# A two-layer network with causal attention on one core: the short score packs of two sequences in column tiles in one PSUM bank, and the sending of probabilities placed between the two halves of the query move

## The chip, the core and the metric

The kernel runs on one core of a Trainium2 chip. The metric is device time in microseconds (us), one launch, float32 throughout. An execution has five engines that each work through their own queue in order: TensorE (PE in the profile; PEld is its weight load), VectorE (DVE), ScalarE (ACT), GpSimd (POOL), and SyncE (SP), which here only issues transfers. Data lies in SBUF (128 partitions); matmuls write PSUM, eight banks of 128 x 512 float32.

## The reference, cut to what matters

Two layers act on 16 sequences of 256 tokens with 256 features. The first (a linear recurrence gated by an MLP) is not touched by the change. The second multiplies an attention output by a gate and adds it to x:

```python
q = (x @ Wq).reshape(B, S, 16, 192)          # 128 "nope" + 64 rotated columns per head
c_kv, k_rope = split(x @ Wkv_a, [64])        # 64 latent + 64 rotated columns, shared by all heads
k, v = expand(rmsnorm(c_kv) @ Wkv_b)         # per head
scores = einsum('bqhd,bkhd->bhqk', q, k) / sqrt(192)
scores = where(tril, scores, -max)
out = einsum('bhqk,bkhd->bqhd', softmax(scores), v) @ Wo
x = x + out * silu(base(x) + lora(x))
```

The kernel folds the expansion of the keys into the query weights, so a score is a product over 128 numbers: 64 latent and 64 rotated ones (two rotated halves of 32). All heads share the same keys of a sequence.

## The kernel before, in words

Tokens are worked in 8 chunks of 512, that is two sequences (b = 0 and 1) each. In the second layer a chunk has 16 heads in 4 groups of 4. A *unit* is one group of heads and one sequence; there are 64 units, and the main loop runs over them: step i works on unit i, sequence 0 in even steps and sequence 1 in odd ones. r is the step's place in its chunk (0 to 7). Units 2n and 2n+1 make group n.

**Scores.** The 256 queries of a sequence are cut into 8 blocks of 32. Block a of 4 heads is one matmul with 4 x 32 = 128 weight columns; because of the causal mask it meets only the first 32(a+1) keys. The 8 matmuls go in three packs, each into one PSUM bank (`PACK`): blocks 7 and 6; blocks 5, 4 and 3; blocks 2, 1 and 0, which have 96, 64 and 32 columns. The three packs of a unit are spread over its step (`score_pack`, lines 1671, 1706 and 1722), with other matmuls between them. A float32 matmul is two passes, so that pack 2 of a unit is 6 instructions at full width. From unit 6 on, the even units do pack 2 differently: each block as two matmuls with 64 weight columns, one for the lower and one for the upper half of the output partitions (`halves`), 12 instructions, marked 128\*64 in the profile. Odd units do pack 2 at full width. After the matmuls of a pack, DVE adds the mask and takes the row maxima (`nm`), ACT takes exponentials into a buffer `pr` (one for even, one for odd units) and sums the rows (`sr`); later DVE takes the reciprocals and POOL multiplies (`normalise`): packs 0 and 1 at the end of the step, pack 2 at the start of the next. The pool of score banks has 3 banks, that of all other matmul outputs 5.

**Probabilities.** The next step transposes them on DVE (`turn`, three calls; the last, `turn(w, 0)`, stands after pack 1 of the step). `send` (4 transfers) writes them to memory outside the core (`far`), and `fetch` reads them back as `pT` with the heads arranged for the product with the values: per group 4 fetches, (y, b) for key half y and sequence b. `values_of(n)` multiplies both sequences of a group at once, 32 matmuls in quarters of the array (64\*64), first with y = 0, then with y = 1. It stands in even step 2n + 4, after pack 1. So group n is sent in steps 2n+1 (sequence 0) and 2n+2 (sequence 1), fetched in steps 2n+2 and 2n+3, and used in step 2n+4.

**Queries.** Group n is projected in steps 2n-3 and 2n-2 (`query_mm`); POOL combines the rotated halves (`query_rot`, tile `qrot`), and `query_move` copies them to partitions 64 to 127 of `qg` with 8 transfers, 4 for each rotated half. This stands first in even step 2n-2, and the scores of group n begin in step 2n.

**The SP queue.** Moves, sends and fetches of the main loop are all issued by SP, in program order; each waits for what it needs before the next is issued. In an even step the order is: 8 moves, fetch (0, 0), 4 sends of the odd unit before, fetch (1, 0); in an odd step: fetches (0, 1) and (1, 1), then 4 sends of the even unit.

PE's order is the program's: a manual dependency chains each instruction to the one before it. After the last step a tail computes the last products and writes the last rows.

Of the kernel before, what the change touches and what calls it, by code (L numbers as in the profile page):

```python
# [11 lines left out]
F32 = mybir.dt.float32  # L12
# [6 lines left out]
P = 128  # L19
B, S, D = 16, 256, 256  # L20
NTOK = B * S
CH = 512
# [19 lines left out]
def tile_two_layers(ctx: ExitStack, tc: tile.TileContext, d: dict, out: bass.AP):  # L42
# [54 lines left out]
    pe = InOrder(nc.tensor)  # L97
# [132 lines left out]
    chunks = [Chunk() for _ in range(NCH)]  # L230
# [150 lines left out]
    NQ = S // 32  # L381
# [4 lines left out]
    groups = [Group() for _ in range(NCH * NG)]  # L386
# [40 lines left out]
        gp.tensor_tensor(q.rot[:, 0, :], m0[:, 0, :], m1_[:, 1, :], ALU.subtract)  # L427
        gp.tensor_tensor(q.rot[:, 1, :], m1_[:, 0, :], m0[:, 1, :], ALU.add)

    def query_move(n):  # L430
        q = groups[n]
        for r in range(2):
            for h in range(G):
                sp.dma_start(
                    q.qg[64 + 32 * r : 96 + 32 * r, :, h, :],
                    q.rot[32 * h : 32 * h + 32, r, :].rearrange("p (a q) -> p a q", q=32),
                )


    with ExitStack() as l0:  # L440
# [106 lines left out]
        def tiny(name, n=1):  # L547
            return w0.tile([P, n], F32, tag=name, name=name)
# [43 lines left out]
        u = tiny("u")  # L592
        f = tiny("f")
# [24 lines left out]
        for k in range(8):  # L618
            n = 1 << k
# [112 lines left out]
        def recur_in(ch, pb):  # L732

            v = a2.tile([P, S], F32, tag="v", name=f"v_{ch}")
            w = a2.tile([P, S], F32, tag="w", name=f"w_{ch}")
            v0.tensor_tensor(v, pb, ct, ALU.mult)
            swapped(w, pb)
            return v, w
# [8 lines left out]
        def recur_out(ch, g, w, ve, ge):  # L747

            swapped(w, g)
            h = a2.tile([P, S], F32, tag="hs", name=f"hs_{ch}")  # L750
            ve.tensor_tensor(h, g, ct, ALU.mult)
            ge.tensor_tensor(h, h, w, ALU.subtract)
            return h
# [478 lines left out]
        o = out1  # L1232
        for ch in range(FIRST, NCH - 1):
            xn, xnT, norm2, o = middle(ch, xn, xnT, norm2, fill, o)
# [25 lines left out]
        v, w = recur_in(ch, recur_mm(ch, xnT, ps_mm))  # L1260
# [7 lines left out]
        h = recur_out(ch, g, w, v0, g0)  # L1268
# [33 lines left out]
    ps_sc = ctx.enter_context(tc.tile_pool(name="ps_sc", bufs=3, space=PSUM))  # L1302
# [37 lines left out]
    PACK = (((7, 0), (6, 256)), ((5, 0), (4, 192), (3, 384)), ((2, 0), (1, 96), (0, 192)))  # L1340
# [12 lines left out]
    for t in prs:  # L1353
        for a in range(NQ):
            w = 32 * (a + 1)
# [3 lines left out]
    class Unit:  # L1359


        def __init__(self, i):
            self.i = i
            self.ch, r = divmod(i, 2 * NG)
            self.g, self.b = divmod(r, 2)
            self.n = f"{self.ch}_{self.g}_{self.b}"
            self.pr = prs[i % NPR]

    def score_pack(u, pi):
        k, b, pack = chunks[u.ch], u.b, PACK[pi]  # L1370
        if pi == 0:
            u.nm = sm1.tile([P, NQ], F32, tag="nm", name=f"nm_{u.n}", bufs=3)
            u.sr = sm1.tile([P, NQ], F32, tag="sr", name=f"sr_{u.n}", bufs=3)
        qg = groups[u.i // 2].qg
        sc = ps_sc.tile([P, CH], F32, tag="sc", name=f"sc_{u.n}_{pi}")
        halves = 2 if pi == 2 and u.b == 0 and u.i > 4 else 1
        m = P // halves
        for a, o in pack:
            w = qg[:, b * NQ + a, :, :].rearrange("p h q -> p (h q)")
            for y in range(halves):  # L1380
                pe.matmul(
                    sc[m * y : m * y + m, o : o + 32 * (a + 1)], w[:, m * y : m * y + m],
                    k.kT[:, b * S : b * S + 32 * (a + 1)], start=True, stop=True,
                )
        ends = [o + 32 * (a + 1) for a, o in pack]
        step = ends[1] - ends[0]
        n = len(pack)
        assert ends == [ends[0] + step * z for z in range(n)]
        if ends[0] - 32 + step * n <= CH:
            diag = sc[:, ends[0] - 32 : ends[0] - 32 + step * n].rearrange("p (n s) -> p n s", n=n)[:, :, 0:32]  # L1390
        else:
            diag = sc[:, ends[0] - step : ends[-1]].rearrange("p (n s) -> p n s", n=n)[:, :, step - 32 : step]
        ve.tensor_tensor(diag, diag, bc(kmask, n), ALU.add)
        for a, o in pack:
            ve.tensor_reduce(
                u.nm[:, a : a + 1], sc[:, o : o + 32 * (a + 1)], AX.X, ALU.max, negate=True
            )
        for a, o in pack:
            w = 32 * (a + 1)
            ac.activation(  # L1400
                u.pr[:, OFF[a] : OFF[a] + w], sc[:, o : o + w], AF.Exp,
                bias=u.nm[:, a : a + 1], accum_out=u.sr[:, a : a + 1],
            )

    def normalise(u, packs):
        blocks = [a for pi in packs for a, _ in PACK[pi]]
        lo, hi = min(blocks), max(blocks) + 1
        ve.reciprocal(u.sr[:, lo:hi], u.sr[:, lo:hi])
        for a in blocks:
            v = u.pr[:, OFF[a] : OFF[a] + 32 * (a + 1)]  # L1410
            gp.tensor_scalar(v, v, u.sr[:, a : a + 1], 1.0, ALU.mult, ALU.mult)
# [32 lines left out]
    def fetch(n, y, b):  # L1444

        q = groups[n]
        if y == b == 0:
            q.pT = {}
        if b == 0:
            q.pT[y] = pp.tile([P, G, 3 * P], F32, tag="pT", name=f"pT_{n}_{y}", bufs=3)  # L1450
        sp.dma_start(
            q.pT[y][64 * b : 64 * b + 64].rearrange("p h q -> p (h q)"),
            q.far[b].rearrange("(y k) s h z q -> y (k s) (h z q)", y=2)[y],
        )
# [197 lines left out]
    units = [Unit(i) for i in range(LAST)]  # L1652
    for i in range(LAST):
        ch, r = divmod(i, PER)
        odd = i % 2 == 1
        u, w = units[i], units[i - 1] if i else None
        here = w is not None and w.i >= LAST - 2
        n = (i + 3) // 2 if odd else (i + 2) // 2
        n = n if n < len(groups) else None
        more = ch + 1 < NCH  # L1660
        last = ch - 1 if ch == NCH - 1 and r in FINISH else None
        fast = ch - 1 if 0 < ch < NCH - 1 else None

        if not odd and n is not None:
            query_move(n)
        if odd and i > 2:
            fetch((i - 3) // 2, 0, 1)
            fetch((i - 3) // 2, 1, 1)
        elif i and not odd:
            fetch((i - 2) // 2, 0, 0)  # L1670
        score_pack(u, 0)
        if w:
            normalise(w, (2,))
        if fast is not None and r > 3:
            fast_begin(fast, r)
        if ch > 1 and r == 0:
            fast_begin(ch - 2, 0)
        out_weights(i)
        if r == 1:
            gate_end(ch, 0)  # L1680
        if r == 2:
            gate_end(ch, 1)
            if more and ch:
                norm_end(ch + 1)
        if r == 5 and more:
            kv_end(ch + 1)
        if i == LAST - 1:

            finish_mm(last, 3, 0, NPAIR)
            finish_out(last, 3)  # L1690
            last = None
        if w:
            for z in (1, 2):
                turn_here(w, z) if here else turn(w, z)

        if r == 0:
            mid_chunk(ch)
        if r == 7 and more:
            key_chunk(ch + 1)
        if n is not None:  # L1700
            query_mm(n, 0 if odd else 3)
            if not odd:
                query_lat(n, 3)
        if i == 5:
            values_of(0)
        score_pack(u, 1)

        if odd and n is not None:
            query_mm(n, 1)
            query_mul(n, 0)  # L1710
        if w:
            if here:
                turn_here(w, 0)
            else:
                turn(w, 0)
                send(w)
        if not odd:
            if i > 4:
                values_of((i - 4) // 2)
            if i:  # L1720
                fetch((i - 2) // 2, 1, 0)
        score_pack(u, 2)
        normalise(u, (0, 1))

        if odd and n is not None:
            query_mm(n, 2)
            query_mul(n, 1)
            query_rot(n)
            query_lat(n, 2)
        if r < 2:  # L1730
            gate_begin(ch, r)
        if r == 0 and more and ch:
            norm_begin(ch + 1)
        if r == 2 and more:
            transpose_chunk(ch + 1)
        if r == 4 and more:
            kv_begin(ch + 1)
        if r == 6 and more:
            router_chunk(ch + 1)
        if last is not None:  # L1740
            j = FINISH.index(r)
            finish_mm(last, j, 0, NPAIR)
            finish_out(last, j)
        if fast is not None and r in FINISH:
            fast_end(fast, r)
# [1 line left out]

    ch = NCH - 1
    u0, u1 = units[LAST - 2], units[LAST - 1]
    normalise(u1, (2,))  # L1750

    finish_mm(ch, 0, 0, 4)
    finish_mm(ch, 1, 0, 4)
# [86 lines left out]
```

## Time and profile before

| | us |
|---|---|
| median of 3 runs | 906.04 (905.31 to 906.72) |
| the profiled execution | 903.67 |
| its span, first to last instruction | 901.9 |
| PE busy | 889.3 (99%) |
| DVE, POOL, ACT busy | 667.4, 571.2, 476.0 |
| first score matmul | at 266.5 |
| last score matmul | at 877.2 |

The span is from the first to the last instruction that the profile records; the execution's own time is 1.8 us longer. A group's line gives operation, output and inputs, the shape, the count, then busy time, mean duration in ns and the idle time before. Matmuls overlap in a pipeline: a duration is not what a matmul adds to the queue, which is the distance from its start to the start of the next. So costs on PE are read from starts in the timeline. The mean granted clock of PE over the span is 0.994.

### The profile page before, as it was taken

To read this page: it belongs to the slowest core of one execution; us is meant where nothing else is said; L and a number is where in the kernel's file an instruction comes from. 1 tells how busy PE (TensorE), PEld (TensorE's weight loads), DVE (VectorE), ACT (ScalarE), POOL (GpSimd) and SP (SyncE) were. 2 spreads that over 40 slices of the span, in tenths; PEclk is the share of its full clock that TensorE was granted. 3 is DMA by queue.
4 is the path that set the end of the run, shared out by engine and by line. 5 is a ranking of instruction groups with operands and counts; after the bars stand their busy time and mean duration, and the time that the engine had idled before them with its cause. 6 is when DMAs were issued, how large, how long until landed. Compare 5 with 4: busy or idle time off the path is not lost.

```text
span 901.9 us, 17976 instructions
## 1 busy us (share of the span) xinstructions
PE 889.3 (99%) x5688; PEld 666.8 (74%) x5688; DVE 667.4 (74%) x2017; ACT 476.0 (53%) x1562; POOL 571.2 (63%) x885
## 2 busy tenths in 40 slices
PE   9999999999999989999999999999999999999988
PEld 8777999987757657776776777677677767766766
DVE  6886678764687869678868867886886788687642
ACT  3234665644436646655655565565556556556441
POOL 2229687787355537787586677758667775876531
PEclk9999999999999999999999999999999999999989
DMA  9730000000024888887887887788788768878880
GB/s 276 245 118 1 1 2 1 1 1 1 1 32 79 230 209 198 186 207 161 217 218 169 206 181 201 180 217 214 170 200 211 190 170 209 210 176 194 209 223 29
DMA packets 197406, 134.04 MB, mean 149 GB/s; under 512 B 143104, under 2 KB 187968, under 8 KB 197312
## 3 DMA queue, kind: packets, MB, share of 16 engines
q1 hardware_dynamic: 195184, 128.69, 58.0%
q0 software_dynamic: 1152, 3.67, 1.2%
q8 instruction: 46, 0.75, 0.4%
q10 hardware_dynamic: 976, 0.53, 0.2%
q14 instruction: 48, 0.39, 0.1%
HBM read 63.11 MB, written 52.95 MB: 129 GB/s over the span
## 4 chain that ended last, share of the span: by engine, by line
PE 93%; DVE 3%; DMA 2%; POOL 1%; ACT 1%; SPq 0%; issue 0%; ACTq 0%; POOLq 0%
PE pq L53 23%; PE sc L53 14%; PE po L53 11%; PE av L53 8%; PE f L53 7%; PE r L53 7%; PE pg L53 5%; PE ph L53 5%; PE pf L53 5%; PE pm L53 2%; PE pkv L53 2%; PE tp L53 2%; DMA far<-turned 1%; DMA pT<-far 1%; PE pb L53 1%; PE py L53 1%
## 5 line engine op out<-in xcount | busy, mean ns | idle before, releaser
L53 POOL TENSOR_SCALAR pr<-pr,sr 128x256 f32<-128x256 f32 (+7 forms) x512 | 192.5, 397 | 188.2 <-DVE sr L53 180.3
L53 ACT ACTIVATE pr<-sc,nm 128x256 f32<-128x256 f32 (+7 forms) x512 | 190.2, 382 | 217.1 <-DVE sr L53 139.6
L53 PEld LDWEIGHTS sc<-kT,qg 128*128 128x128 f32 (+1 forms) x1198 | 150.8, 176 | 54.8 <-issue 41.6
L53 PE MATMUL sc<-kT,qg 128*128 128x32 f32 (+6 forms) x1198 | 169.0, 290 | 0.0
L53 DVE TENSOR_REDUCE nm<-sc 128x1 f32<-128x256 f32 (+7 forms) x512 | 127.5, 301 | 6.6
L53 DVE STREAM_TRANSPOSE turned<-pr 128x512 f32<-128x512 f32 x186 | 123.2, 687 | 11.0 <-POOL pr L53 10.9
L53 PE MATMUL pq<-xnT,wlat 128*128 128x512 f32 x256 | 122.7, 602 | 0.0
L53 PE MATMUL pq<-xnT,wrope 128*128 128x512 f32 x256 | 120.2, 593 | 0.0
L53 ACT ACTIVATION_READ_ACCUMULATOR pr<-sc,nm 128x1 f32 x512 | 104.0, 203 | 0.0
L53 PE MATMUL av<-pT,rowv 64*64 64x512 f32 (+2 forms) x992 | 80.5, 445 | 6.0 <-DMA pT<-far 6.0
L53 POOL TENSOR_TENSOR qrot<-qmul,qmul 128x512 f32<-128x512 f32 x64 | 83.6, 1329 | 2.8 <-DVE qmul L53 2.8
L53 DVE TENSOR_TENSOR sc<-sc,kmask 128x96 f32<-128x96 f32 (+1 forms) x192 | 45.2, 236 | 53.8 <-PE sc L53 52.5
L53 DVE TENSOR_TENSOR qmul<-pq,rot_q 128x512 f32<-128x512 f32 x128 | 80.7, 672 | 0.1
L53 ACT ACTIVATE qg<-pq 64x512 f32<-64x512 f32 x128 | 75.5, 590 | 4.3 <-PE pq L53 3.5
L53 PEld LDWEIGHTS av<-pT,rowv 64*64 64x64 f32 x992 | 39.8, 135 | 43.6 <-issue 30.1
L53 PEld LDWEIGHTS pq<-xnT,wrope 128*128 128x128 f32 x256 | 45.7, 191 | 32.4 <-issue 32.1
L53 PEld LDWEIGHTS pq<-xnT,wlat 128*128 128x128 f32 x256 | 45.7, 191 | 31.6 <-issue 31.6
L53 PEld LDWEIGHTS po<-wout,attT 128*128 128x128 f32 x416 | 59.3, 193 | 9.8 <-issue 3.5
L53 PE MATMUL po<-wout,attT 128*128 128x128 f32 (+1 forms) x416 | 65.3, 311 | 0.0
L53 POOL TENSOR_TENSOR attT<-attT,attT 128x512 f32<-128x512 f32 x36 | 45.1, 1273 | 0.0
L53 POOL TENSOR_TENSOR rs<-ve,mhalf 128x4 f32<-128x4 f32 (+1 forms) x17 | 16.8, 987 | 41.1 <-DVE ve L53 33.6
L53 PE MATMUL pf<-p2T,hT 128*128 128x256 f32 x192 | 42.7, 380 | 0.0
(229 smaller groups left out, 1520.0 us busy)
## 6 DMA issues: line engine op xcount, KB each, us to landing
far<-turned SPq DMA_DIRECT2D x248, 192.0 KB, 4.4
pT<-far SPq DMA_DIRECT2D x124, 384.0 KB, 4.9
qg<-qrot SPq DMA_DIRECT2D x256, 64.0 KB, 2.7
x<-in_x_dram SPq DMA_DIRECT2D x7, 512.0 KB, 10.4
out_dram<-x POOLq DMA_DIRECT2D x12, 256.0 KB, 4.0
wqn_wo<-in_wq_nopeT_dram SPq DMA_DIRECT2D x4, 512.0 KB, 5.4
wqn_wo<-in_Wo_dram SPq DMA_DIRECT2D x4, 512.0 KB, 6.8
p2T<-in_proj2T_dram SPq DMA_DIRECT2D x2, 512.0 KB, 8.3
```

Source lines behind the costliest of these rows:

```text
L53: r = getattr(self.engine, name)(*args, **kw)
```

## The change

`score_pack` is cut into its matmuls (`score_mm`) and the rest (`score_exp`). Pack 2 is always done with 64 weight columns, and in the even step for both sequences: 24 matmuls one after the other into one score bank (columns 0 to 191 and 256 to 447), then mask, maxima and exponentials of both. The odd steps have no pack 2. `normalise` of pack 2 is done for both sequences at the start of the odd step, and its call in the tail is gone. `query_move` takes the rotated halves to move as an argument: half 0 stays first in the even step, half 1 comes after `send`; fetch (0, 0) comes after it.

```diff
-    def query_move(n):
+    def query_move(n, part=(0, 1)):
         q = groups[n]
-        for r in range(2):
+        for r in part:
             for h in range(G):
                 sp.dma_start(
...
-    def score_pack(u, pi):
-        k, b, pack = chunks[u.ch], u.b, PACK[pi]
-        if pi == 0:
+            self.nm = None
+
+    def score_mm(u, pi, sc, base=0):
+        k, b = chunks[u.ch], u.b
+        qg = groups[u.i // 2].qg
+        m = P // 2 if pi == 2 else P
+        for a, o in PACK[pi]:
+            w = qg[:, b * NQ + a, :, :].rearrange("p h q -> p (h q)")
+            for y in range(0, P, m):
+                pe.matmul(
+                    sc[y : y + m, base + o : base + o + 32 * (a + 1)], w[:, y : y + m],
+                    k.kT[:, b * S : b * S + 32 * (a + 1)], start=True, stop=True,
+                )
+
+    def score_exp(u, pi, sc, base=0):
+        if u.nm is None:
             u.nm = sm1.tile([P, NQ], F32, tag="nm", name=f"nm_{u.n}", bufs=3)
             u.sr = sm1.tile([P, NQ], F32, tag="sr", name=f"sr_{u.n}", bufs=3)
...
+        pack = [(a, base + o) for a, o in PACK[pi]]
...
+    def score_pack(u, pi):
+        sc = ps_sc.tile([P, CH], F32, tag="sc", name=f"sc_{u.n}_{pi}")
+        score_mm(u, pi, sc)
+        score_exp(u, pi, sc)
+
+    def score_small(u, v):
+
+        sc = ps_sc.tile([P, CH], F32, tag="sc", name=f"sc_{u.n}_2")
+        for z, y in enumerate((u, v)):
+            score_mm(y, 2, sc, z * S)
+        for z, y in enumerate((u, v)):
+            score_exp(y, 2, sc, z * S)
...
-        if not odd and n is not None:
-            query_move(n)
         if odd and i > 2:
             fetch((i - 3) // 2, 0, 1)
             fetch((i - 3) // 2, 1, 1)
-        elif i and not odd:
-            fetch((i - 2) // 2, 0, 0)
+        if not odd and n is not None:
+            query_move(n, (0,))
         score_pack(u, 0)
-        if w:
+        if odd:
             normalise(w, (2,))
+            normalise(u, (2,))
...
         if not odd:
+            if n is not None:
+                query_move(n, (1,))
+            if i:
+                fetch((i - 2) // 2, 0, 0)
             if i > 4:
                 values_of((i - 4) // 2)
             if i:
                 fetch((i - 2) // 2, 1, 0)
-        score_pack(u, 2)
+            score_small(u, units[i + 1])
         normalise(u, (0, 1))
...
     u0, u1 = units[LAST - 2], units[LAST - 1]
-    normalise(u1, (2,))
```

More of the change, by code (lines that the diff above doesn't have):

```diff
@@ L1367, in __init__ @@
             self.pr = prs[i % NPR]
-    def score_pack(u, pi):
-        k, b, pack = chunks[u.ch], u.b, PACK[pi]
-        if pi == 0:
+            self.nm = None
[12 more added lines that the diff above has]
+        if u.nm is None:
             u.nm = sm1.tile([P, NQ], F32, tag="nm", name=f"nm_{u.n}", bufs=3)
             u.sr = sm1.tile([P, NQ], F32, tag="sr", name=f"sr_{u.n}", bufs=3)
[L1374 to L1384, printed above, removed]
+        pack = [(a, base + o) for a, o in PACK[pi]]
         ends = [o + 32 * (a + 1) for a, o in pack]
```

## The prediction

> **What bounds the kernel now.** First the busy times and the chain that ended last, then PE's timeline in a chunk, then who waited for whom, then the clock, and last SP's timeline.
>
> ```profile
> PE 889.3 (99%) x5688; PEld 666.8 (74%) x5688; DVE 667.4 (74%) x2017; ACT 476.0 (53%) x1562; POOL 571.2 (63%) x885
> PE 93%; DVE 3%; DMA 2%; POOL 1%; ACT 1%; SPq 0%; issue 0%; ACTq 0%; POOLq 0%
> ```
>
> PE sets the time: what leaves its queue leaves the span, unless a new wait takes its place. Its timeline in steps 33 (odd) and 34 (even, r = 2), start and duration:
>
> ```profile
> 584.39 0.75 PE L53 MATMUL sc<-kT,qg 128*128 128x96 f32 x6
> 584.98 1.96 PE L53 MATMUL pq<-xnT,wlat 128*128 128x512 f32 x4
> 586.78 1.03 PE L53 MATMUL pg<-wbase,xnT 128*128 128x256 f32 x4
> ...
> 592.80 2.67 PE L53 MATMUL av<-pT,rowv 64*64 64x512 f32 x32
> 595.40 0.59 PE L53 MATMUL sc<-kT,qg 128*64 128x96 f32 x12
> 595.92 1.09 PE L53 MATMUL tp<-ident,xn 128*128 128x128 f32 x8
> ```
>
> By starts, pack 2 at full width takes 0.59 us (584.39 to 584.98), and the four pq after it 1.80 where the same four after another wide matmul take 1.71 (580.14 to 581.85): 0.67 us in all. In column tiles it takes 0.52 (595.40 to 595.92). The same 12, cut off after 2, 4 and 8:
>
> ```profile
> 595.40 0.30 PE L53 MATMUL sc<-kT,qg 128*64 128x96 f32 x2
> 595.40 0.39 PE L53 MATMUL sc<-kT,qg 128*64 128x96 f32 x4
> 595.40 0.50 PE L53 MATMUL sc<-kT,qg 128*64 128x96 f32 x8
> ```
>
> Ends come 0.09 us apart for a pair of 96 columns, 0.055 for 64, and 0.09 for both pairs of 32 (0.50 to 0.59). Much of the 0.52 is the way in and out.
>
> ```profile
> PE av L53 <- DMA pT<-far: 6.0, 3, 3.1
> 319.22:322.63 3.41, 2.72 (x22) 1.51 (x24) 0.71 (x1) 0.37 (x3) 0.19 (x1) 0.50 1.02 298
> 865.35:872.17 6.82, 6.69 (x33) 4.80 (x34) 1.88 (x9) 2.88 (x12) 2.76 (x8) 0.50 0.68 199
> ```
>
> PE's only long waits are for fetched probabilities, in steps 6 and 62. After each the granted clock (third from the end in the stretches) is 0.50, for 3.41 and 6.82 us. The 32 value matmuls take 2.31 us by starts where nothing is late; from 315.77 to 323.54 they take 7.77, from 859.95 to 867.39 7.44.
>
> ```profile
> 592.19 6.82 SPq L53 DMA_DIRECT2D qg<-qrot  x8
> 599.05 0.63 SPq L53 DMA_DIRECT2D pT<-far  x1
> 599.78 2.75 SPq L53 DMA_DIRECT2D far<-turned  x4
> 602.63 4.26 SPq L53 DMA_DIRECT2D pT<-far  x3
> 606.99 2.85 SPq L53 DMA_DIRECT2D far<-turned  x4
> ...
> 596.63 0.70 DVE L53 STREAM_TRANSPOSE turned<-pr 128x512 f32<-128x512 f32 x1
> ...
> far<-turned SPq DMA_DIRECT2D x248, 192.0 KB, 4.4
> pT<-far SPq DMA_DIRECT2D x124, 384.0 KB, 4.9
> qg<-qrot SPq DMA_DIRECT2D x256, 64.0 KB, 2.7
> ```
>
> SP hardly rests. The send could go at 597.33, when the last transpose ends, but stands behind eight moves and a fetch until 599.78; the fetches of sequence 1 then wait for its landing.
>
> **The change part by part.** The sum is against the profiled execution, 903.67 us (span 901.9 and 1.8 around it), 2.4 below the median; I apply it to the median.
>
> *Matmuls.* 32 odd packs at 0.67 go: -21.4. 32 packs join the even ones. Such a pack pays no way in or out: 2 x 0.09 + 2 x 0.055 + 0.09 = 0.38, of which 0.02 or so is the last pass with nothing behind it; I take 0.36, +11.5. Ends: 0.52, if it pays its own way in and out; 0.32, streaming alone (384 columns at the 0.43 us per 512 of the pq rows, two tiles at once). Together **-9.9** (-4.8 to -11.2). Three early even packs change from 0.67 to about 0.62: nothing.
>
> A rule speaks against the 32-column passes: the Trainium skill, "TensorEngine Tiling (Array Packing)", section "Instruction Overhead", puts some 60 cycles on each matmul, so that short ones cost alike, and says not to take a tiling factor from a dimension that is small already. The rows show 0.045 for a pair of 32 against 0.055 for 64; by the rule both would be 0.055, 32 x 0.02 = 0.6 less gained, and the total 895.6 for 895.0.
>
> *Send before the late half of the moves, step 34.* Send from 597.4, 2.75 us, to 600.1; four moves at 0.79 (a row of eight at 6.33) to 603.3; two fetches at 0.63, and by then (600.1 + about 4) the send has landed, so the other two go on to 605.9 instead of 606.89. But now four fetches stand in a row. Two in a row land 1.7 apart (the values resume at 863.81 and 865.48). First landing 603.3 + 4.9 = 608.2, third 611.6, fourth 613.3. The values of step 36 began at 611.32 and did not wait; PE now comes 0.3 to 0.7 earlier and needs the third at once and the fourth 1.35 later. The transposes end some 0.2 earlier too (one reciprocal less before them). A wait of 0.4 to 1.2; I take 0.8, in the six chunks (1 to 6) whose r = 2 has the normalisation on DVE that makes the transposes late: **+4.8** (0, if fetches overlap; 12, a further landing interval each).
>
> *The other steps.* In r = 0 the last transpose waited 0.88 for POOL's pack 2, now done a step earlier; seven value groups that took up to 2.8 instead of 2.31 (2.60 in the row above), 2.0 in all, come to 0.8: **-1.2** (-2.0 to +2). At r = 4 and 6 the group has 2 us and more in hand.
>
> *Late half of the moves.* It lands about 5.3 after the first issue when behind a send (the same halves at 592.19 needed 6). Step 34: 600.1 to 605.4, needed at 607.2: free. In chunk 0, with no values yet, steps are short: transposes end 289.3, send to 292.0, landing 297.3, and step 4's first score wants it at 295.9: 1.4. In step 6 likewise 1.1 (the fourth early move waits for a fetch eight transfers before it). **+2.5** (0 to 5).
>
> *Step 6.* Fetches go at 311.6 to 314.2 and land as late as before (319.9, 321.6), but PE arrives 1.5 later, at 317.3: a wait of 3.0 instead of 5.46 with its half clock (3.41 at 0.50 is 1.7). **-2.5** (-5.5 to +0.5).
>
> *Step 62.* Transposes of unit 59 end at 847.65, the send went at 852.80. Now it goes at once: late half to 853.6, third landing 853.6 + 4.9 + 3.4 = 861.9, fourth 863.6, PE there at 859.6: 2.7 instead of 5.1, and the 4.8 us at half clock after it, 2.4, should go. **-4.8** (-7.5 to 0).
>
> *Engines beside PE.* Instructions on ACT, DVE and POOL stay 1:1, but six exponentials come in the even step. The reciprocal of the odd unit's pack 2 stands in the odd step ahead of the transposes, and waits in r = 3 for three exponentials more, 1.0 us; behind it are transposes, qmul and, through POOL, the next early half. SP then waits for the odd unit's transposes, 3 us later, anyway. A score bank is taken again three packs later, one step or more after its exponentials. Nothing, up to 0.2 a pair: +6. POOL's 3 multiplications per pair move to the odd step, where it idles 4 us (before 605.12); the tail's go with PE's order ahead: nothing.
>
> Sum: -9.9 + 4.8 - 1.2 + 2.5 - 2.5 - 4.8 = -11.1. **906.0 - 11.1 = 895.0.**
>
> **Rivals.** *No new waits* (0.17): fetches in a row overlap, early moves land in time: -9.9 - 1.2 - 2.5 - 4.8 = -18.4, **887.6**. For it: transfers of one row spread over all queues, whose share here is 0.80 and not 1. Against: the 1.7 us between landings.
>
> *The joined pack pays in full* (0.10), 0.52 as it does alone: 32 x 0.16 = 5.1 less, **900.1**. Against: the pace inside the 12.
>
> *Slower* (0.09): the four fetches in a row come so late at r = 4 that PE idles about 3 us and the clock falls, as it did in step 6. Six times 3.0 + 1.7 is 28 instead of 4.8: +12, **918**. It decides where the wait passes 0.8 + 11.1 / 6 = 2.65 us. For it: the values there had no slack. Against: it needs another whole landing interval.
>
> *No effect* (0.05): SP and the transfers set the pair's length and PE's gain turns into waits everywhere, 906. For it: SP's rows are contiguous. Against: 2.4 us of the fetch row (4.26 for three that take 0.63) are waits that the change removes.
>
> **How the numbers follow.** The main case has 0.59; with its own terms moving by 4 it spans 891 to 899. The range 886 to 903 takes in the first two rivals and leaves the slower one and tails out. Faster (by over 0.2%, 1.8 us, about what can be told) 0.86, same 0.04, slower 0.10.
>
> **What would show it.** 1408 score matmuls instead of 1198; 24 in column tiles, about 0.88 us by starts; two pq pairs adjoining in odd steps; sends starting within 0.2 us of the last transpose in r = 2; four fetches in a row; values about 3 us by starts in the steps with r = 4 of chunks 1 to 6, else 2.31; small waits before steps 4 and 6; no 0.50 clock after step 62. Wrong it would be if the 24 take over 1.0, if PE waits for score banks or for ACT in odd steps, or if the values of r = 4 take over 4.

## The result and the profile after

The changed kernel takes 915.43 us (median of 6 runs, 913.9 to 917.21), the kernel before, run beside it, 905.51 (903.37 to 906.72). The ratio is 1.0117, with a 95% interval of 1.0101 to 1.0133: 10 us slower, where 11 us faster was forecast. The profiled execution of the changed kernel took 917.21 us; its span is 915.4, for 901.9 before.

First the busy times, and the engines' shares of the chain that ended last:

```profile
PE 891.8 (97%) x5898; PEld 658.5 (72%) x5898; DVE 669.3 (73%) x2017; ACT 474.8 (52%) x1562; POOL 570.9 (62%) x885
PE 63%; DMA 11%; DVE 11%; SPq 9%; POOL 2%; ACT 2%; issue 2%; DVEq 0%; ACTq 0%; POOLq 0%
```

Before, PE had 93% of that chain; now 31% of it belongs to transfers, DVE and SP's queue. PE alone no longer sets the length of a chunk. Its timeline in steps 32 (even, r = 0) and 33 and at the start of step 34 (start, duration, operation, count, then the idle time before and its releaser):

```profile
580.98 2.38 PE L53 MATMUL av<-pT,rowv 64*64 64x512 f32 x32
583.30 0.99 PE L53 MATMUL sc<-kT,qg 128*64 128x96 f32 x24
584.22 1.13 PE L53 MATMUL pg<-wbase,xnT 128*128 128x256 f32 x4
...
589.44 0.98 PE L53 MATMUL sc<-kT,qg 128*128 128x192 f32 x6
590.25 1.88 PE L53 MATMUL pq<-xnT,wrope 128*128 128x512 f32 x4
591.97 1.88 PE L53 MATMUL pq<-xnT,wlat 128*128 128x512 f32 x4
...
599.72 1.08 PE L53 MATMUL av<-pT,rowv 64*64 64x512 f32 x4
602.12 2.42 PE L53 MATMUL av<-pT,rowv 64*64 64x512 f32 x28 [1.33 <-DMA pT<-far]
604.47 0.70 PE L53 MATMUL sc<-kT,qg 128*64 128x96 f32 x14
```

The matmuls do what they should. By starts the 24 take 0.92 us (583.30 to 584.22), 0.40 more than the 12 did, and the odd step, where two pq groups now adjoin (590.25, 591.97), is 0.67 shorter: 0.27 us less per pair of steps, 8.6 over 32 pairs. But in step 34 the values, which begin at 599.72, are done at 604.47: 4.75 us for 2.31. I call the difference to 2.31 their *lateness* (the waits inside the row, and what a lower clock behind them adds): here 2.44. Over all 31 groups it sums to 28.3 us, for 12.7 before.

PE's list of waits (us in total, times, longest) has small new ones as well:

```profile
PE av L53 <- DMA pT<-far: 10.6, 9, 2.2
PE pq L53 <- DVE qmul L53: 1.6, 6, 0.3
PE sc L53 <- DMA qg<-qrot: 1.6, 2, 0.8
```

The largest change is in the waits of DVE, which the prediction did not read:

```profile
DVE sc L53 <- ACT pr L53: 46.5, 32, 2.3
```

This row did not exist before. DVE's timeline at the end of step 32 shows what it is:

```profile
584.28 0.70 DVE L53 STREAM_TRANSPOSE turned<-pr 128x512 f32<-128x512 f32 x1
584.90 0.23 DVE L53 TENSOR_TENSOR sc<-sc,kmask 128x96 f32<-128x96 f32 x1
585.17 0.48 DVE L53 TENSOR_REDUCE nm<-sc 128x1 f32<-128x96 f32 x3
587.59 0.27 DVE L53 TENSOR_TENSOR sc<-sc,kmask 128x96 f32<-128x96 f32 x1 [1.93 <-ACT pr L53]
587.88 0.49 DVE L53 TENSOR_REDUCE nm<-sc 128x1 f32<-128x96 f32 x3
```

The first mask and maxima are sequence 0's. The mask is a write into the score tile, and sequence 1's mask goes into the same tile, so it waits until ACT has read sequence 0's scores for its exponentials, though the columns are others: the trace shows it waiting for a semaphore (a counter by which one engine releases another) that ACT counts up with its exponentials. With the wait the small pack holds DVE from 584.90 to 588.4; the two masks and two groups of maxima alone take some 1.5 us.

What is late next can be read from POOL's rotation and SP's timeline around it:

```profile
582.36 2.50 POOL L53 TENSOR_TENSOR qrot<-qmul,qmul 128x512 f32<-128x512 f32 x2
```

```profile
583.65 3.49 SPq L53 DMA_DIRECT2D qg<-qrot  x4
587.24 3.27 SPq L53 DMA_DIRECT2D far<-turned  x4
590.61 2.74 SPq L53 DMA_DIRECT2D qg<-qrot  x4
593.39 2.54 SPq L53 DMA_DIRECT2D pT<-far  x4
596.48 2.19 SPq L53 DMA_DIRECT2D far<-turned  x4
```

The rotation of r = 0 starts 5.8 us into the step (576.60); before it was 3.7 (573.64, step 32 from 569.92). SP's early moves wait for it, and everything behind them goes late: the send, though its transposes ended at 584.98, the late moves, and at 593.39 four fetches in a row, for values due at 599.72.

To see where time went, I took the difference between PE's step lengths in two traces, less what the matmuls explain (-0.67 an odd step, +0.40 an even one), and summed it by the place in the chunk. Times are counted from the start of step 0, and all sums go up to the start of step 63. The first row is the change; the others are pairs of kernels explained below (us; "ends" are steps 6 and 62). Each row compares two single executions.

| | score matmuls | r = 0 | r = 2 | r = 4 | ends | odd steps | step 63 begins later by |
|---|---|---|---|---|---|---|---|
| changed, against before | -8.0 | +2.8 | +16.5 | +3.4 | -2.6 | +3.4 | +15.6 |
| maxima first, SP of before, against before | -8.0 | -0.2 | +7.3 | +0.7 | +2.2 | +0.3 | +2.3 |
| the same with gate product on POOL, against before with that | -8.0 | +0.3 | +5.7 | +0.1 | +1.4 | 0.0 | -0.5 |
| the same with a shorter router (*again*), against before with that | -8.0 | 0.0 | +0.6 | +0.7 | +4.9 | 0.0 | -1.8 |

The 3.4 us of odd steps in the first row lie in chunk 0 alone: two waits for late moves, which lengthen steps 3 and 5, and one of 1.3 us for keys that ACT writes, at the end of step 7.

### The profile page after: what moved, and what is told of

Read it like the earlier page. It is cut to its first block, busy times and chain, and to the rows that moved or that the text cites. A ratio compares the mean times of both kernels' runs of the same rounds, so it can differ in the third digit from the quotient of the medians.

```text
span 915.4 us, 18211 instructions
## 1 busy us (share of the span) xinstructions
PE 891.8 (97%) x5898; PEld 658.5 (72%) x5898; DVE 669.3 (73%) x2017; ACT 474.8 (52%) x1562; POOL 570.9 (62%) x885
## 4 chain that ended last, share of the span: by engine, by line
PE 63%; DMA 11%; DVE 11%; SPq 9%; POOL 2%; ACT 2%; issue 2%; DVEq 0%; ACTq 0%; POOLq 0%
PE pq L53 13%; DMA pT<-far 10%; SPq L53 9%; PE po L53 8%; PE sc L53 7%; PE f L53 7%; PE r L53 7%; PE av L53 5%; PE pf L53 5%; PE ph L53 5%; DVE turned L53 3%; DVE nm L53 3%; DVE qmul L53 2%; PE pkv L53 2%; POOL pr L53 2%
## 5 line engine op out<-in xcount | busy, mean ns | idle before, releaser
L53 PEld LDWEIGHTS sc<-kT,qg 128*64 128x64 f32 (+1 forms) x1408 | 136.5, 163 | 44.5 <-issue 30.9
L53 PE MATMUL sc<-kT,qg 128*64 128x96 f32 (+7 forms) x1408 | 157.4, 277 | 2.8 <-DMA qg<-qrot 1.6
L53 PE MATMUL pq<-xnT,wlat 128*128 128x512 f32 x256 | 120.6, 594 | 1.6 <-DVE qmul L53 1.6
L53 DVE TENSOR_TENSOR sc<-sc,kmask 128x64 f32<-128x64 f32 (+1 forms) x192 | 46.3, 241 | 103.5 <-PE sc L53 56.8
L53 PE MATMUL av<-pT,rowv 64*64 64x512 f32 (+2 forms) x992 | 89.8, 450 | 12.3 <-DMA pT<-far 10.6
L53 PEld LDWEIGHTS pq<-xnT,wlat 128*128 128x128 f32 x256 | 48.0, 190 | 48.9 <-issue 45.0
L53 PE MATMUL ph<-xnT,p1T 128*128 128x256 f32 (+1 forms) x128 | 42.6, 487 | 0.0
```

The lines of the kernel that those rows point to most:

```text
L53: r = getattr(self.engine, name)(*args, **kw)
```

## The experiments

All ratios are to runs of the kernel before on the same chip in the same sitting, with 95% intervals. Theory A, formed from the profile above: the change joins two independent things, a shared score tile that makes DVE wait, and a new order on SP; each delays the values. Rivals: the bank itself is what two engines collide on; or the shorter PE steps are useless whatever the rest does.

**1. The order on SP alone, in the kernel before.**

```diff
-            query_move(n)
+            query_move(n, (0,))
...
                 send(w)
+            query_move(n, (1,))
+            fetch((i - 2) // 2, 0, 0)
```

> The kernel before with the order of SP's queue alone changed (early half of the moves, send, late half, four fetches). Shared-bank theory (the change is slow because DVE's mask of the second sequence waits for ACT's exponentials in the same bank, 46.5 us in 32 waits, and transposes and qrot come late): no such wait here, so within 3 us of before, 902 to 909 us; the values of r = 2 take under 3 us by starts. Queue theory (the change is slow because four fetches in a row behind the late half land too late): slower by 8 us or more, 913 and up, with values of 4 to 5 us in r = 2, as in the changed kernel.

1.0039 (1.0016 to 1.0062): slower. The lateness of the values is 17.6 us in its trace (12.7 before), 4.8 of it in the six groups of r = 2 in steps 18 to 58 (1.3 before). The time, 909.56 us, lies between the two forecasts. The order that sends as soon as the transposes allow is a loss by itself.

**2. The joined packs alone, with SP in the order of before** (8 moves and fetch (0, 0) at the start of the even step).

```diff
-            query_move(n, (0,))
+            query_move(n)
...
-            query_move(n, (1,))
-            fetch((i - 2) // 2, 0, 0)
```

> The changed kernel with SP's order of before: column tiles of both sequences in one bank, 8 moves and fetch (0, 0) ahead of the send. Shared-bank theory: the 32 DVE waits of about 1.45 us stay, and the send still stands behind moves that wait for a late qrot: no faster than before, 905 to 916 us. Queue theory: PE's 32 x 0.27 = 8.6 us are gained and the waits are those of before: 895 to 899 us.

1.0060 (1.0039 to 1.0082). The joined packs lose too, as the shared-bank theory forecast (911.57 us), and DVE's waits for ACT stand as they were:

```profile
DVE sc L53 <- ACT pr L53: 46.6, 32, 2.3
```

**3 and 4. The small packs of the two sequences in two banks**, once with SP's new order and once with the old.

```diff
-        sc = ps_sc.tile([P, CH], F32, tag="sc", name=f"sc_{u.n}_2")
+        scs = [ps_sc.tile([P, CH], F32, tag="sc", name=f"sc_{y.n}_2") for y in (u, v)]
```

> The changed kernel with pack 2 of the two sequences in two banks of the pool of three. Shared-bank theory: DVE's waits for ACT are gone, transposes and qrot come 1 to 2 us earlier, most of the waits for fetches go: 895 to 902 us. Queue theory: the four fetches stay in a row, 910 us or more.

> Two banks, and SP's order of before: only PE's work moves. Both theories: PE's 8.6 us less with about the waits of before, 895 to 900 us. If PE's gain only turns into waits for transfers (the rival that PE does not set the pair's length), 904 us or more.

1.0027 (1.0011 to 1.0043) and 1.0003 (0.9979 to 1.0027). DVE's wait for ACT is gone from both traces. Neither time is what the theories forecast: 907.99 us lies between the two, and 906.60, for which both had 895 to 900, is where the rival had put it (904 or more). Beside experiment 2, from the same sitting, the shared tile costs 911.57 - 906.60 = 5.0 us.

**5 and 6. One bank, but masks and maxima of both sequences before the exponentials of both**, again with both orders on SP. This keeps the bank and takes away only the order of writes and reads.

```diff
-        for z, y in enumerate((u, v)):
-            score_exp(y, 2, sc, z * S)
+        packs = [score_max(y, 2, sc, z * S) for z, y in enumerate((u, v))]
+        for y, pack in zip((u, v), packs):
+            score_act(y, pack, sc)
```

> The changed kernel, with masks and maxima of both sequences ahead of the exponentials of both; still one bank, still SP's new order. If DVE's 32 waits for ACT come from the order of reads and writes on one tile and not from the bank itself, they are gone: 906 to 910 us, as with two banks (907.99). If the bank itself serves one engine at a time, 913 and up.

> The same with SP's order of before. One bank leaves a third score bank free, so the early waits for a bank that two banks showed (1.5 us) go: 903 to 906 us. If waits in r = 2 eat the gain of PE whatever the banks, as in two_banks_old_sp (values 0.8 to 1.7 us late there), not under 903.

1.0059 (1.0042 to 1.0076) and 0.9992 (0.9970 to 1.0015); 908.29 us is in the forecast for the order of writes and reads (906 to 910). DVE's timeline with the new order on SP, same step:

```profile
580.84 0.23 DVE L53 TENSOR_TENSOR sc<-sc,kmask 128x96 f32<-128x96 f32 x1
581.11 0.49 DVE L53 TENSOR_REDUCE nm<-sc 128x1 f32<-128x96 f32 x3
581.63 0.27 DVE L53 TENSOR_TENSOR sc<-sc,kmask 128x96 f32<-128x96 f32 x1
581.93 0.48 DVE L53 TENSOR_REDUCE nm<-sc 128x1 f32<-128x96 f32 x3
```

The second mask follows at once, in the same bank, and waits for ACT no longer. So the wait comes with the order of writes and reads on one tile. Whether two engines could work in one bank at the same time is not tested by this: ACT's first exponential of these packs starts at 582.53, after DVE's last maxima (582.41), so the two do not meet. The price of SP's new order in this pair is 908.29 - 903.66 = 4.6 us. With both undone, the joined packs are as fast as before and no faster: theory A explains the loss, but not where the 8.6 us are. The second row of the table says: at r = 2 (+7.3) and in step 6 (+2.2, with 6.83 us at half clock in this trace and 3.41 in that of before).

Theory B: in r = 0 the rotation, and behind it moves, send and fetch, keep a pace that DVE and POOL set, so that PE, being faster, waits for the values of r = 2. POOL's row before the rotation, in step 31 and 32, first of before and then of the version of experiment 6:

```profile
566.94 0.90 POOL L53 TENSOR_SCALAR pr<-pr,sr 128x96 f32<-128x96 f32 x3 [5.31 <-DVE sr L53]
567.81 1.27 POOL L53 TENSOR_TENSOR c<-c,g 128x512 f32<-128x512 f32 x1
569.15 1.27 POOL L53 TENSOR_TENSOR x<-x,c 128x512 f32<-128x512 f32 x1
...
571.64 2.03 POOL L53 TENSOR_SCALAR pr<-pr,sr 128x256 f32<-128x256 f32 x5
573.64 2.50 POOL L53 TENSOR_TENSOR qrot<-qmul,qmul 128x512 f32<-128x512 f32 x2
```

```profile
568.33 1.78 POOL L53 TENSOR_SCALAR pr<-pr,sr 128x96 f32<-128x96 f32 x6 [4.42 <-DVE sr L53]
570.06 1.27 POOL L53 TENSOR_TENSOR c<-c,g 128x512 f32<-128x512 f32 x1
...
573.81 2.03 POOL L53 TENSOR_SCALAR pr<-pr,sr 128x256 f32<-128x256 f32 x5
575.82 2.50 POOL L53 TENSOR_TENSOR qrot<-qmul,qmul 128x512 f32<-128x512 f32 x2
```

POOL idles, waits for DVE's reciprocal, and from there works up to the rotation with no gap over 0.3 us. DVE in turn has a row from the router to that reciprocal (the router is the small network in the gate that picks two experts; DVE works it for the next chunk in r = 6 and 7). The first row shown is the router's last wait for PE, the second the reciprocal, in the kernel before and in experiment 6:

```profile
560.45 0.17 DVE L53 TENSOR_TENSOR lg<-pm,rb_bc 128x16 f32<-128x16 f32 x1 [0.75 <-PE pm L53]
...
566.61 0.17 DVE L53 RECIPROCAL sr<-sr 128x3 f32<-128x3 f32 x1
```

```profile
562.10 0.17 DVE L53 TENSOR_TENSOR lg<-pm,rb_bc 128x16 f32<-128x16 f32 x1 [0.29 <-PE pm L53]
...
568.00 0.23 DVE L53 RECIPROCAL sr<-sr 128x3 f32<-128x3 f32 x2
```

Between these rows DVE waits for 0.1 us in the second trace. There the rotation starts 4.9 us into r = 0 (570.90) for 3.7 before. Of these 1.2 us, 0.4 are POOL's later start against the step (2.57 us ahead of it for 2.98): DVE's row begins 8.80 us ahead of the step for 9.47, because PE's odd step is 0.67 shorter, and is itself 0.26 shorter. The other 0.8 are POOL's row, 7.49 us for 6.70, since the change put three more multiplications (0.88 us) at its head.

**7. Send and fetch (1, 0) before the 8 moves, in r = 0 only** (in the version of experiment 6).

```diff
-        if not odd and n is not None:
+        if not odd and r and n is not None:
             query_move(n)
...
                 send(w)
+            if not r and n is not None:
+                query_move(n)
```

> max_first_old_sp, and in r = 0 alone the 8 moves stand behind the send and both first fetches. There the send stood 5 to 6 us behind moves that wait for a late qrot. If this chain (qrot, moves, send, fetch, values of r = 2) is what eats PE's gain, about 1 us per chunk comes back: 896 to 901 us, values of r = 2 at 2.31 to 2.8 us. If transfers as a whole set the pair, the wait moves to the scores of r = 2 (late moves) and nothing is gained: 903 us or more.

1.0112 (1.0070 to 1.0154). The values of r = 2 have no lateness left (0.0 in steps 18 to 58), but the scores of r = 2, which need the moves, do, and behind such a wait the granted clock (third number from the end) falls, three times in this trace; once in step 34:

```profile
PE sc L53 <- DMA qg<-qrot: 9.6, 5, 2.7
```

```profile
596.00:599.40 3.40, 3.35 (x6) 2.19 (x7) 1.33 (x4) 0.29 (x1) 2.49 (x2) 0.51 0.95 222
```

Either the values or the scores wait, as the second forecast had it: what SP must issue in r = 0 behind a late rotation does not fit.

**8 to 10. Less work on DVE between router and rotation.** Seven instructions of the router, 1.6 us of DVE a chunk, are left out (the gate then keeps one expert, so these kernels show where time goes and are no versions to use), with joined packs (twice, in two sittings) and in the kernel before.

```diff
-        l2 = t3("l2")
-        ve.scalar_tensor_tensor(l2, oh1, -3e38, lg, ALU.mult, ALU.add)
-        _, oh2 = first_max(l2, 2)
-        ve.tensor_tensor(oh1, oh1, oh2, ALU.add)
```

> max_first_old_sp with the router's second maximum left out (the gate keeps the first expert alone): 7 small DVE operations per chunk, about 1.6 us of DVE in r = 6 and 7, nothing on PE. If DVE's row of work from r = 6 to the qmul of r = 7 sets when qrot comes and so the wait in r = 2, that wait falls by about 1 us per chunk: 896 to 900 us. If not, the time is that of max_first_old_sp within 1.5 us.

> The kernel before with the router's second maximum left out, as in no_second_max (the gate keeps the first expert only, so the output is not the reference's): 7 instructions of VectorE, 1.6 us, less in each chunk, the small packs not joined. no_second_max, with joined packs, had 0.9919. If the 8.6 us less of score matmuls can be had once VectorE is less late, this one gains only what the small waits of before gave (0.1 to 0.45 us in six chunks): 0.996 to 0.999, and no_second_max stays 4 to 7 us below it. If the gain of no_second_max was VectorE's alone and TensorE's gain goes into waits even then: within 2 us of no_second_max, 0.990 to 0.994.

> no_second_max as it was, to stand beside the run above on one chip: 0.989 to 0.995 by both theories. By the first it is 4 to 7 us below before_no_second_max, by the second within 2 us of it.

With joined packs 0.9919 (0.9889 to 0.9949) and 0.9942 (0.9919 to 0.9966); not joined, beside the second of these, 0.9957 (0.9935 to 0.9978). The rotation of r = 0 moves to 3.9 us, and the lateness at r = 2 falls from 7.4 us to 1.6 and 0.6 over steps 18 to 58: theory B holds. But the joined packs are only 2.7 us ahead (895.45 to 898.18), with overlapping intervals: between the two forecasts. The table's last row shows where the rest may be. In chunks 1 to 6 PE gains 5.5 us, nearly all of 6.5, and steps 6 and 62 take 4.9 back. In step 62 PE reaches the values 5.1 us earlier, while sequence 1's fetches land only 2.8 and 3.3 us earlier, and PE has 10.2 us at half clock in the two steps for 3.4. How much of this is the chance of one execution is open: in the trace of the same kernel from the other sitting, against the same trace of before, chunks 1 to 6 gain 3.6 us and steps 6 and 62 take 2.6 back.

**11 and 12. The product with the gate on POOL** (0.69 us on DVE a chunk, 1.06 on POOL, which idles at that point), with joined packs and in the kernel before.

```diff
-        ve.tensor_tensor(m3, m3, bc_in(gate.rearrange("p j e -> p (j e)"), LR), ALU.mult)
+        (gp if ch else ve).tensor_tensor(m3, m3, bc_in(gate.rearrange("p j e -> p (j e)"), LR), ALU.mult)
```

> The version with masks and maxima of both first and SP in the order of before (max_first_old_sp, 0.9992), with one instruction moved: the router's multiplication of the 128 x 512 hidden values by the gate, 0.69 us on VectorE in r = 6 and 7, is made by GpSimd for chunks 1 to 7. If the fetched probabilities of r = 2 are late because VectorE works without a pause from the router to the rotation's products, and SP's moves, send and fetch of r = 0 stand behind that: GpSimd's rotation in r = 0 starts some 0.6 us earlier (4.2 to 4.4 us into the step for 4.9), the values of r = 2 wait 0.5 to 1.1 us less in each of six chunks, and the time falls by 3 to 6 us, to a ratio of 0.993 to 0.997: below the kernel before and the changed one. Rival: SP's own row of transfers sets r = 0 and r = 2, whatever VectorE does: no gain, 0.999. Third: GpSimd, which has its normalisation to do in the same steps, takes so long over it that its rotation comes later: 1.000 to 1.005.

> The kernel before with that one instruction moved to GpSimd and nothing else. There the values of r = 2 were late by 0.1 to 0.45 us only, so little can be gained: 0.997 to 1.000. If it gains as much as max_first_old_sp does by it (0.995 or less), then the lateness of VectorE is no consequence of the shorter PE steps but was there before.

0.9961 (0.9945 to 0.9977) and 0.9971 (0.9944 to 0.9997). Both beat the kernel before, by 3.5 and 2.6 us by these ratios, and are equal within the intervals; the rotation of r = 0 starts 4.2 us in with joined packs, as forecast. PE's waits for fetched probabilities, joined and not joined:

```profile
PE av L53 <- DMA pT<-far: 6.7, 2, 3.5
```

```profile
PE av L53 <- DMA pT<-far: 4.8, 2, 2.5
```

The list leaves the many small ones out; by starts the lateness is 18.7 us against 10.0 in these two traces. That difference, 8.7, is as much as the matmuls gain. I had expected little of this edit without joined packs (0.997 to 1.000), and it came out at the edge of that: there the lateness of r = 2 fell from 1.3 to 0.0, and by 2.7 us in all.

**13. The router two steps earlier, where DVE has idle time.**

```diff
-        if r == 4 and more:
+        if r == 3 and more:
             kv_begin(ch + 1)
-        if r == 6 and more:
+        if r == 4 and more:
             router_chunk(ch + 1)
```

`kv_end` moves from r = 5 to r = 4.

> max_first_old_sp with the router of the next chunk two steps earlier, in r = 4, where VectorE idled 4.0 us, and, to make room for its tile, the preparation of the keys of the next chunk begun in r = 3 and ended in r = 4 for r = 4 and 5. All instructions stay. If VectorE's unbroken row from r = 6 to r = 7 makes the values of r = 2 late: that row loses some 4 us, the rotation of r = 0 starts at 3.7 us into the step or earlier, the values of r = 2 wait under 0.5 us as where the second maximum was left out, and the ratio is 0.990 to 0.994, though nothing is left out. If what helped there was the missing work as such: 0.998 to 1.001. What may go wrong: in r = 4 the row on VectorE delays the products for the queries, and scores or values of r = 6 become late: 1.000 to 1.010.

1.0004 (0.9973 to 1.0034). The rotation of r = 0 starts 2.3 us in, and the lateness of r = 2 is 0.0 in all chunks; step 6's is 0.4. But PE then waits elsewhere, for the output products that follow in r = 4 and 5, and once, in step 8, the values were 7.1 us late with 10 us at half clock:

```profile
PE po L53 <- POOL attT L53: 3.6, 6, 1.0
PE po L53 <- ACT qg L53: 2.6, 2, 1.3
```

So the cause is confirmed at its place, and the version gains nothing: of the forecasts it fits the one of what may go wrong, at other steps than named.

**14 and 15. Four of the eight moves of r = 0 issued by ScalarE**, with and without joined packs.

```diff
+        split = r == 0 and ch
         if not odd and n is not None:
-            query_move(n)
+            query_move(n, (0,) if split else (0, 1))
...
             score_small(u, units[i + 1])
+            if split:
+                query_move(n, (1,), ac)
```

> mid_pool (0.9961) with the late four of the eight moves of r = 0 of chunks 1 to 7 issued by ScalarE, behind its exponentials of the small packs, instead of SyncE: ScalarE idled 2.0 us there (579.2 to 581.2 in the trace of mid_pool), SyncE's row of eight took 6.7 us. If SyncE's row behind the late rotation is what makes the values of r = 2 late: the send of r = 0 goes 3 us earlier, within 2.5 us of its last transpose for 5 to 6, the values of r = 2 wait under 0.3 us in every chunk for 0.6 to 1.25, and the time falls by 4 to 7 us more, to a ratio of 0.989 to 0.992. Rival: the issues hold ScalarE up by some 0.8 us each, the exponentials of r = 1 come 1 to 2 us later, and sends and values of r = 2 with them: 0.996 to 1.000.

> before_mid_pool (0.9971) with the same four moves on ScalarE. Its values of r = 2 had no wait left, so nothing is gained: 0.997 to 1.000. With moves_act it tells whether the 8.6 us that leave TensorE's queue can be had at all: if they were hidden only by the late fetches of r = 2, moves_act is 4 to 8 us below this kernel; if the fetches of steps 6 and 62 and other waits take them as well, the two stay within 3 us.

1.0049 (1.0029 to 1.0069) and 1.0019 (0.9999 to 1.0039). Neither forecast came out: SP's row got shorter, but its send went later, not earlier. SP's timeline and its waits in step 32 with joined packs:

```profile
582.45 3.19 SPq L53 DMA_DIRECT2D qg<-qrot  x4
585.75 0.56 SPq L53 DMA_DIRECT2D pT<-far  x1
591.27 2.22 SPq L53 DMA_DIRECT2D far<-turned  x4
```

```profile
SPq L53 <- DMA qg<-qrot: 4.9, 1, 4.9
```

The send waited 4.9 us for one of the moves to land, though it does not use their data. In the trace each transfer signals its end on one of eight semaphores taken in turn, and ScalarE's moves, issued from 586.32 on, hold four of them. The first of the four sends takes the semaphore of ScalarE's first move, which landed at 591.21; that this reuse is the reason is read from the trace and was not tried. The pair therefore does not tell what it was made for.

**16 and 17. The even unit's three multiplications back in the even step**, in the version of experiment 6 and in that of 11.

```diff
         if odd:
-            normalise(w, (2,))
             normalise(u, (2,))
...
         normalise(u, (0, 1))
+        if not odd:
+            normalise(u, (2,))
```

> max_first_old_sp (0.9992) with the reciprocal and the three multiplications of the even unit's small pack at the end of the even step instead of the start of the odd one; the odd unit's stay. In the trace of max_first_old_sp GpSimd works without a pause from 568.33, where it takes six of these multiplications (1.78 us; three, 0.90 us, in the kernel before), to the rotation at 575.82. If the three that the change moved into this row are part of what makes the rotation late: it starts 0.4 to 0.9 us earlier (4.0 to 4.5 us into r = 0 for 4.9), the values of r = 2 wait about that much less in six chunks, and the ratio is 0.994 to 0.997. If VectorE's row alone sets it: VectorE now waits some 0.3 us for ScalarE's exponentials before the router, the rotation comes no earlier, and the ratio is 0.999 to 1.002.

> mid_pool (0.9961; the multiplication by the gate on GpSimd) with the same move. Both together take 0.4 to 0.9 us off GpSimd's row and had taken 0.7 off VectorE's: the rotation 3.4 to 3.9 us into r = 0 as in no_second_max, the values of r = 2 within 0.3 us of their time, and 0.991 to 0.995, with the whole computation. Since the fetches of steps 6 and 62 come no earlier, some 4 us of TensorE's 8.6 go into longer waits there, as they did in no_second_max_again. If the two gains do not add, 0.996.

1.0015 (1.0001 to 1.0030) and 0.9956 (0.9938 to 0.9973): the first is the rival's case, the second that of gains that do not add. POOL's row is 0.9 us shorter, as intended, but DVE, which takes the reciprocal before the router, now waits for ACT:

```profile
562.86 0.18 DVE L53 RECIPROCAL sr<-sr 128x3 f32<-128x3 f32 x1 [1.05 <-ACT pr L53]
```

Its row begins later, POOL's with it, and the rotation starts 4.7 to 4.8 us into the step for 4.9. A shorter row behind a later start brings nothing. The three versions with the gate product on POOL and all moves on SP lie within each other's intervals (0.9956 to 0.9971); the lowest median ratio is this one's, 0.4% below the kernel before.

## Why the prediction was wrong, step by step

- **The matmuls: right, but for the size.** -8.6 for -9.9: the second dozen takes 0.40, not 0.36. By ends, its first pair of 96 columns takes 0.11 for 0.09, and the 0.02 that I took off for the last pass is not saved. The rule cited from the Trainium skill ("TensorEngine Tiling (Array Packing)", "Instruction Overhead") would have given, by the estimate worked out from it, some 0.6 less than my sum; the measured shortfall is 1.3. It does not lie in the 32-column passes, though: their two pairs take 0.09 us by their ends in the second dozen as they did before. Another bullet of that page speaks more to this case: its section "PSUM Bottleneck" says that tiling speeds up TensorE but not the work that empties PSUM. What is left with both mistakes undone agrees in kind: PE has less to do, DVE and POOL have not, and the ratio is 0.9992. DVE's 46.5 us of new waits are something else, an order of instructions and no lack of speed.
- **"Engines beside PE ... Nothing" failed.** I asked when a score bank comes free again, not who reads and writes inside one tile. The new DVE row, 46.5 us in 32 waits, is worth 5.0 us (experiments 2 and 4). I had even priced a wait (0.2 a pair at most) for "three exponentials more" at the reciprocal in the odd step; it sat in the even step, at the mask, 1.45 us long on average, and ahead of the router and the query products.
- **"POOL's 3 multiplications ... where it idles 4 us ... nothing" failed as well.** The idle time lies before DVE's reciprocal; behind it POOL's row has no gap over 0.3 us up to the rotation, so in r = 7 the three lengthen it by 0.8 us. What they cost by themselves is not shown: experiment 16 takes them out of the row and gains nothing, because the row then begins later.
- **"The other steps", -1.2: wrong sign, and the largest miss.** r = 2 alone has +16.5, of which 7.3 stay with both mistakes undone, through the values of groups that are sent in r = 0. I took DVE and POOL to move with PE. They do not: DVE idles 0.4 us in r = 7 (step 31, experiment 6), so that PE's odd step gets 0.67 shorter and DVE's row only 0.26.
- **The four fetches in a row: right, but mostly at the wrong place.** I put +4.8 on r = 4, 0.8 in each of six chunks. The lateness there is 3.3 us in all, but 2.6 of it in step 12 (376.36 to 381.32, 4.96 us by starts) and at most 0.5 in the others. That one step passed the 4 us which I had named as a sign of being wrong; why chunk 1 differs is open. The fetches are late behind r = 0, where the rotation holds the early moves and so the send. SP's order costs 0.4% alone and 4.6 us with the joined packs.
- **Step 6: right.** Lateness 3.5 for 3.0 predicted, and no half clock. **Step 62: wrong.** 4.8 as before (5.1), not 2.7, with 3.41 us at half clock: the first fetch was issued 5.6 us before the values, about as forecast (6.0), but the third landed 8.8 us after that, not 8.3, and the clock fell all the same.
- **Late half of the moves in chunk 0: right in kind,** 1.6 us in two waits for 2.5.
- **The sends at once: right in r = 2 of chunks 1 to 6,** within 0.03 us of the last transpose (2.2 us behind it in step 58), and worth nothing.

Of the rivals the one at 0.05, that PE's gain turns into waits, names the mechanism that is left when both mistakes are undone: 0.9992. The slower rival had the four fetches, at another step; that its 918 lies near the measured 915 is luck, since it had 28 us of lateness at r = 4 and the trace has 3.3.

What stays open: how much of the 8.6 us could be had. With the shorter router, 5.5 of 6.5 us appeared in the middle chunks of one trace and 3.6 in another. No run took away the waits of both step 6 and step 62, and experiment 13, which nearly removed step 6's, got a longer one in step 8. The gain of the joined packs with the shorter router (2.7 us) is within the intervals.

## What to carry to other kernels

Read the waits of every engine that will write or read a tile which the change makes common, and look for a write that comes after another engine's read in program order: here it cost a wait though the columns lay apart, and writing all before reading any removed it. An engine at 99% is worth shortening only where the others have idle time behind it: take each stage, find the engine without a gap, and see whether its work gets shorter too. Idle time counts as cover only if it lies after the wait that holds the engine, not before it.

## What the runs showed that I had not expected

- One product of 128 x 512 moved from DVE (0.69 us) to POOL (1.06) in seven chunks took 2.7 us of lateness out of the kernel before and made it 0.3% faster: DVE's row in r = 7, on an engine that is 74% busy, was already on the path.
- A transfer on a second queue can hold up the first: SP's send stood 4.9 us until a move of ScalarE had landed that it had no use for (by the reuse of a semaphore, as read from the trace).
- The length of one wait did not tell whether the clock falls. In the changed kernel's trace a wait of 1.46 us in step 50 is followed by 6.83 us at half clock, the one of 2.14 in step 6 by none (first and second row). The stretches at half clock in the main loop lasted 3.41, 6.83 or 10.24 us:

```profile
320.36 2.70 PE L53 MATMUL av<-pT,rowv 64*64 64x512 f32 x28 [2.14 <-DMA pT<-far]
...
762.13 4.01 PE L53 MATMUL av<-pT,rowv 64*64 64x512 f32 x28 [1.46 <-DMA pT<-far]
```

```profile
762.70:769.53 6.83, 6.83 (x59) 5.09 (x52) 3.38 (x11) 3.01 (x14) 0.00 (x0) 0.50 0.99 250
```
